# Loading an expert's matrices in two parts: w1 and w2 three tiles ahead, w3 two tiles ahead

## The chip, the cores and the metric

The kernel runs on one core of one Trainium2 chip. The metric is device time in microseconds (us) for one execution of the whole program; the time of a kernel is the median of its runs.

## What is computed

Two layers work on 3327 rows of 256 numbers. Each has an attention over a graph and a feed-forward part. The change lies in the feed-forward part of layer 0, a mixture of 16 experts of which each row uses the best two. Cut to that part, the reference is:

```python
logits = x @ gate_w + gate_b
top_probs, top_idx = top_k(softmax(logits), 2)          # two experts per row
top_probs = top_probs / sum(top_probs)
hidden = silu(x @ w1[e]) * (x @ w2[e])                   # w1, w2: 256 x 512 for each expert
y = hidden @ w3[e]                                       # w3: 512 x 256
x = x + sum over the two experts of top_probs * y
```

Before it stands layer 0's attention, after it layer 1's attention (softmax over the neighbours, times the projected rows) and a recurrence of 30 steps (tanh, sigmoid, layer norm, a 256 x 256 product).

## The kernel before, in words

The rows that go to one expert are listed and cut into tiles of 128. There are 61 tiles that are always done (`ALWAYS`). The first 16 (`FIRST`) are taken from lists of the first rows, while layer 0's attention and routing are still being finished; their tables are made by `find_tiles` (L670 on) from lists that GpSimd scatters into memory (`list_tokens`, L594). The other 45 come from the complete lists.

For each tile `s`, `work_off` (L909 on) does this. The tile's rows are gathered from memory by GpSimd (L775). They are needed with features first. For the early tiles TensorE transposes them (L804) and ScalarE copies the result to `hT` (L805). For tiles 19 to 60 (`by_dma`) the rows are split into halves of 16 bits by ScalarE (L784), written to memory by GpSimd (`asked`, L789) and read back by a transposing transfer of SyncE, the tile's `face` (L793), which is issued two tiles ahead in program order. Then TensorE makes `hT` times w1 and `hT` times w2 (`product`, L881: 32 matmul instructions), ScalarE and VectorE make `hidden` (L931, L939), and one tile later TensorE multiplies by w3 (`results`, L898: 8 matmul instructions). VectorE scales the result (L902) and GpSimd scatters it to memory (`given`, L903). Where faces are used, TensorE's products are tied to program order: w1 and w2 of tile `s`, then w3 of tile `s-1`.

The matrices of an expert are 3 times 512 KB. There are three sets of buffers (`SETS`): tile `s` uses set `s % 3`. One set is `first_set`, the other two lie in the buffer `wh`. `weights(s)` (L829 on) is SyncE's: it reads the tile's expert number and a flag from a table into registers (L833), and issues the three transfers for w1, w2 and w3 (L841, L842, L843). From tile 3 on each is conditional: it is skipped where the set already holds that expert. Tiles are numbered so that the same expert comes back in the same set.

What sets SyncE's order around the change is the program's order and `issue_after(behind)`: the table read of a set stands behind the last transfer of the set before. In one turn of the loop in `work_off` the queue receives:

```python
if by_dma(s + 2):
    face(s + 2)
if s + SETS - 1 < s1:
    weights(s + SETS - 1)      # w1, w2 and w3 of tile s + 2
```

SyncE works in order. A transfer that refills a buffer waits there until TensorE has read it: w3 of tile `s+2` waits for the results of tile `s-1`, as both use the same set. w1 and w2 of that set were read one tile earlier. Each transfer also waits until the eighth transfer before it (they take turns on eight completion counts, with ScalarE's) has landed.

At the start, set 0 is issued during attention (`begin_tiles`), and set 1 once attention has read the buffer `wh`.

Of the kernel before, what the change touches and what calls it, by code (L numbers as in the profile page):

```python
# [21 lines left out]
P = 128  # L22
# [9 lines left out]
def gat_moe_gat_recurrent_ffn(ctx: ExitStack, tc: tile.TileContext, a: dict, out: bass.AP):  # L32
    nc = tc.nc
# [338 lines left out]
    def score_vectors():  # L372

        for k in range(KD):
            for s in range(2):
                tc.keep_in_program_order(
                    nc.vector.scalar_tensor_tensor(
                        prod, wv1[:, k, 2:], 1.0, va[:, s, :], op0=ALU.mult, op1=ALU.mult,
                        accum_out=wv1[:, k, s : s + 1],
                    )  # L380
                )

    with ExitStack() as moe:
# [28 lines left out]
        with ExitStack() as pre:  # L412
# [58 lines left out]
            behind = None  # L471
# [9 lines left out]
            for ts in groups0[1:3]:  # L481
                behind = take_graph(ts, behind)
# [150 lines left out]
        SETS = 3  # L633
# [133 lines left out]
        def by_dma(s):  # L767
            return FIRST + 3 <= s < ALWAYS
# [28 lines left out]
        def features_first(s):  # L797
            if by_dma(s):
                return faces_of.pop(s)
            row = gotten.pop(s)  # L800
            pt = ps_o.tile([P, 512], F32, name="acc0")[:, :D].rearrange("p (k q) -> p k q", k=KD)
            hT = turn.tile([P, 2, KD, P], F32, name="hT")[:, 0]
            for k in range(KD):
                nc.tensor.transpose(pt[:, k, :], row[:, k * P : (k + 1) * P], ident)  # L804
            nc.scalar.copy(hT, pt)  # L805
            return hT

        behind = None
# [15 lines left out]
                m[:, 2 * third :].rearrange("p (f d) -> p f d", f=FH),  # L824
            )

        ew = {}

        def weights(s):  # L829
            nonlocal behind  # L830

            with tc.issue_after(behind) if behind else ExitStack():
                e, new = nc.values_load_multi_w_load_instructions(  # L833
                    table[0:1, 0:2, s], engines=[mybir.EngineType.SP], min_val=0, max_val=E - 1,
                    skip_runtime_bounds_check_because="numbers of experts, and 0 or 1",
                )[1]
            kw = {} if s < SETS or s in fresh else {"cond": new}
            if s < SETS:
                ew[s] = matrices(s)
            w1, w2, w3 = ew[s % SETS]  # L840
            nc.sync.dma_start(w1, a["w1"][bass.ds(e, 1)].rearrange("e (k p) h -> p (e k) h", p=P), **kw)  # L841
            nc.sync.dma_start(w2, a["w2"][bass.ds(e, 1)].rearrange("e (k p) h -> p (e k) h", p=P), **kw)  # L842
            behind = nc.sync.dma_start(w3, a["w3"][bass.ds(e, 1)].rearrange("e (f p) o -> p (e f) o", p=P), **kw).ins  # L843

        def recurrence_parameters(bank):

# [62 lines left out]
        def work_off(s0, s1, aside):  # L909

            nonlocal tied
            parameters = layer1_parameters()
            hT = features_first(s0)
            made = None
            for s in range(s0, s1 + 1):
                tied = by_dma(s)
                if s == FIRST:
                    for _ in aside:
                        pass
                if s == FIRST + 8:  # L920
                    score_vectors()
                hidT = made
                if s == 1:

                    results(0, hidT)
                if s < s1:
                    for q in range(s + 4 if s <= FIRST else s + 5, min(s + (5 if s < FIRST else 6), s1)):
                        gathered(q)
                    pa = product(hT, ew[s % SETS][0])
                    act, room = edge("e")  # L930
                    silu = nc.scalar.activation(act, pa, AF.Silu).ins  # L931
                    if by_dma(s + 4):
# [6 lines left out]
                    nc.vector.tensor_tensor(made, act, pb, ALU.mult)  # L939
                    if s + 1 < s1:  # L940
                        hT = features_first(s + 1)
                if s > max(s0, 1):
                    results(s - 1, hidT)
                if by_dma(s + 2):
                    face(s + 2)
                if s + SETS - 1 < s1:
                    weights(s + SETS - 1)
                next(aside, None)

        def begin_tiles():  # L950
# [9 lines left out]
        )  # L960
        gathered(3)
        weights(1)


# [19 lines left out]
        fresh = range(ALWAYS, ALWAYS + SETS)  # L984
# [4 lines left out]
        behind = None  # L989
# [280 lines left out]
```

## Time and profile before

| what | value |
|---|---|
| runs of the kernel before | 1831.34, 1831.44, 1829.67 us; median 1831.34 |
| the profiled execution | 1831.93 us, span 1830.2 us, mean granted clock 0.996 |
| transfers | 252.98 MB, mean 138 GB/s |
| experts' stage, 388 to 495 us | TensorE busy 100.97 of 107.00 us, DMA share 0.74, 230 GB/s |
| experts' stage, 495 to 731 us | TensorE busy 236.00 of 236.00 us, DMA share 0.79, 211 GB/s |
| SyncE in 495 to 731 us, waiting at L843 for TensorE's results (L898) | 29.1 us, 23 times |

The span runs from the first to the last instruction on the chip; the profiled execution's own time is 1.7 us longer. All times of single instructions come from this one execution. "Busy" of TensorE (PE) covers pipelined matmuls, so it says that matmuls are in flight, not that they run at their peak. PEld is the loading of the stationary operand, beside PE. "SPq" in a row is SyncE's queue: the duration is that of issuing a transfer, not of moving the data. The DMA share is the mean busy share of the 16 transfer engines. A wait is put down to the instruction whose completion came last; "remote" means that the profile found no instruction to name. L-numbers are lines of the kernel before.

### The profile page before, as it was taken

Reading aid. Unit: us, or ns where it says so; the run is one execution under the profiler, and the core shown is the slowest. Engines: PE = TensorE matmul, PEld = TensorE weight load, DVE = VectorE, ACT = ScalarE, POOL = GpSimd, SP = SyncE. Lnnn points to the kernel's source line nnn. Section 1 sums busy time; section 2 is a strip of 40 time slices with the busy share of each in tenths; the row PEclk is TensorE's granted clock in tenths of the full one; section 3 lists DMA queues with packets and bytes.
Section 4 is the critical chain, followed back from the end, with each engine's and each line's share of the span. In section 5 each row is a group of like instructions: output and inputs, shape, how many; then the busy total and the mean of one; then the engine's idle time right before and its main releaser. Section 6 shows DMA issues by size and latency. Waiting matters only on the chain.

```text
span 1830.2 us, 32461 instructions
## 1 busy us (share of the span) xinstructions
PE 1778.3 (97%) x10896; PEld 1622.7 (89%) x10896; DVE 1318.7 (72%) x4039; ACT 1229.7 (67%) x1587; POOL 914.0 (50%) x702
## 2 busy tenths in 40 slices
PE   6999999999999999799999999999999999999998
PEld 6999999898999999688888878888888888888887
DVE  6888888853222222657676679999999999999998
ACT  2877667642122121456666579999999999999994
POOL 3011212155454542101111028898889889888984
PEclk9999999999999999899999999999999999999999
DMA  8897360257696876400000037777777777767777
GB/s 174 119 125 85 73 102 15 67 168 207 218 264 186 220 203 164 154 15 16 18 22 14 12 91 175 175 166 175 167 168 179 168 177 168 173 166 169 179 168 224
DMA packets 454531, 252.98 MB, mean 138 GB/s; under 512 B 327493, under 2 KB 426620, under 8 KB 454362
## 3 DMA queue, kind: packets, MB, share of 16 engines
q1 hardware_dynamic: 436226, 212.51, 47.1%
q0 software_dynamic: 13456, 33.60, 10.8%
q10 hardware_dynamic: 4680, 4.76, 0.8%
q8 instruction: 89, 1.46, 0.3%
q14 instruction: 80, 0.66, 0.1%
HBM read 168.19 MB, written 97.20 MB: 145 GB/s over the span
## 4 chain that ended last, share of the span: by engine, by line
PE 54%; DVE 4%; DMA 1%; issue 0%; ACT 0%; POOL 0%; SPq 0%; ACTq 0%; DVEq 0%; POOLq 0%
PE po L1177 35%; PE acc L286 14%; PE bank L1142 4%; DVE pT L281 1%; PE acc L163 1%; DMA old<-kept 1%; DVE x L1187 0%; DVE x L1027 0%; DVE stats L1121 0%; DMA given<-wh,to 0%; DVE x L1195 0%; DMA zT<-given 0%; DVE st L116 0%; POOL rstd L121 0%; DVE low L1061 0%
## 5 line engine op out<-in xcount | busy, mean ns | idle before, releaser
L276 ACT ACTIVATE e<-rb,minus,full 128x384 f32<-128x384 f32 (+3 forms) x494 | 399.2, 823 | 168.0 <-DVE pT L281 147.1
L1112 POOL TENSOR_TENSOR th<-th,x 128x1024 f32<-128x1024 f32 (+1 forms) x210 | 464.8, 2213 | 94.3 <-ACT th L1109 86.6
L281 DVE SCALAR_TENSOR_TENSOR pT<-e,part,adjT 128x384 f32<-128x384 f32 (+3 forms) x494 | 383.4, 782 | 118.3 <-PE acc L286 102.3
L1177 PE MATMUL po<-wc,adjT 128*128 128x256 f32 x1888 | 422.2, 379 | 0.0
L1177 PEld LDWEIGHTS po<-wc,adjT 128*128 128x128 f32 x1888 | 356.4, 190 | 47.6 <-DVE x L1187 0.3
L1187 DVE SCALAR_TENSOR_TENSOR x<-po,rr,bb 128x256 f32<-128x256 f32 x780 | 325.0, 477 | 61.6 <-PE po L1177 61.1
L286 PE MATMUL acc<-wh,pT 128*128 128x129 f32 x2704 | 310.7, 276 | 2.1 <-DVE pT L281 2.1
L286 PEld LDWEIGHTS acc<-wh,pT 128*128 128x128 f32 x2704 | 305.4, 192 | 3.2 <-DVE pT L281 2.5
L286 PE MATMUL acc<-s_wh,pT 128*128 128x257 f32 x1352 | 295.5, 381 | 4.0 <-DVE pT L281 4.0
L286 PEld LDWEIGHTS acc<-s_wh,pT 128*128 128x128 f32 x1352 | 255.8, 190 | 43.1 <-DVE pT L281 7.4
L1177 PE MATMUL po<-wc,zT 128*128 128x256 f32 x1232 | 281.0, 379 | 0.6 <-DVE x L1187 0.6
L1121 DVE BATCH_NORM_STATS2 stats<-z 128x6 f32<-128x256 f32 x780 | 274.0, 411 | 1.4 <-ACT z L1116 1.4
L1177 PEld LDWEIGHTS po<-wc,zT 128*128 128x128 f32 x1232 | 229.2, 190 | 29.6 <-issue 0.9
L1152 ACT COPY adjT<-z 128x1024 int16<-128x1024 int16 x236 | 235.2, 1044 | 4.8 <-DVE pT L281 2.0
L121 POOL TENSOR_TENSOR rstd<-ve,neg_half 128x4 f32<-128x4 f32 (+3 forms) x28 | 31.9, 1141 | 411.5 <-DVE ve L119 313.0
L1109 ACT ACTIVATE th<-x 128x1024 f32<-128x1024 f32 (+1 forms) x210 | 209.1, 996 | 28.9 <-DVE x L1187 23.8
L1132 POOL TENSOR_TENSOR rr<-rr,neg_half 128x4 f32<-128x4 f32 (+1 forms) x210 | 206.7, 984 | 26.4 <-DVE rr L1127 26.3
L1116 ACT ACTIVATE z<-th 128x1024 f32<-128x1024 f32 (+1 forms) x210 | 207.1, 986 | 8.3 <-POOL th L1112 2.3
L931 ACT ACTIVATE e<-bank 128x512 f32<-128x512 f32 x61 | 36.4, 597 | 241.0 <-issue 183.2
L939 DVE TENSOR_TENSOR pT<-e,bank 128x512 f32<-128x512 f32 x61 | 41.9, 687 | 190.8 <-PE bank L881 160.7
L903 POOL DMA_INDIRECT given<-wh,to x61 | 61.1, 1001 | 119.2 <-DVE wh L902 102.8
L594 POOL DMA_INDIRECT lists<-pair,ati x52 | 63.5, 1221 | 107.5 <-DVE ati L581 49.3
(202 smaller groups left out, 1731.9 us busy)
## 6 DMA issues: line engine op xcount, KB each, us to landing
wh<-in_w_dram SPq DMA_DIRECT2D x120, 512.0 KB
apart<-adjT SPq DMA_DIRECT2D x236, 256.0 KB
first_set<-in_w_dram SPq DMA_DIRECT2D x63, 512.0 KB
in_bytes<-in_adj_dram POOLq DMA_DIRECT2D x3, 2496.0 KB
asked<-e POOLq DMA_DIRECT2D x42, 128.0 KB
adjT<-apart SPq DMA_TRANSPOSE x236
x<-in_x_dram SPq DMA_DIRECT2D x6, 512.0 KB
kept<-x SPq DMA_DIRECT2D x8, 384.0 KB
```

The costliest lines, as they stand in the source:

```text
L276: nc.scalar.activation(e[:, : n * P], rb[:, : n * P], AF.Relu, scale=sc.full[:, j, h : h + 1], bias=sc.minus[:, j, h : h + 1],)
L281: masked = nc.vector.scalar_tensor_tensor(pT[:, : n * P], e[:, : n * P], sc.part[:, j, h : h + 1], adjT[:, j // 2, ts[0] * P : (ts[-1] + 1 ...
L286: nc.tensor.matmul(po[c], lhsT=pT[:, c * P : (c + 1) * P], rhs=wh[:, j, h, :], start=(j == 0 and c % per_bank == 0), stop=(j == NT - 1), s ...
L1109: self.put(nc.scalar.activation(self.th, self.hs, AF.Tanh, scale=1.0 / S))
L1112: self.put(nc.gpsimd.tensor_tensor(self.th, self.th, self.hs, ALU.add))
L1116: self.put(nc.scalar.activation(self.z, self.th, AF.Silu, scale=1.0 / S))
L1121: self.put(nc.vector.bn_stats(stats[:, j, :], self.z[:, j, :]))
L1132: self.put(nc.gpsimd.tensor_tensor(r, r, neg_half[:, : self.n], ALU.pow))
L1142: nc.tensor.transpose(pt[:, j, k, :], self.z[:, 2 * c + j, k * P : (k + 1) * P], ident)
L1152: self.put(nc.scalar.copy(parts[:, c : c + 2], halves[:, c : c + 2]))
L1177: nc.tensor.matmul(self.po[:, j, :], lhsT=self.zT(j, k), rhs=wc[:, k, :], start=(k == 0), stop=(k == KD - 1),)
L1187: nc.vector.scalar_tensor_tensor(self.hs[:, j, :], self.po[:, j, :], self.r[:, j : j + 1], bb, op0=ALU.mult, op1=ALU.add)
```

## The change

`weights(s)` is divided. `weights_in(s)` reads the table and issues w1 and w2; `weights_out(s)` issues w3, behind whatever the queue had last. In the loop, tile `s` now issues w1 and w2 of tile `s+3` as soon as its own two products and VectorE's product stand in the program, ahead of the face of tile `s+2`; w3 of tile `s+2` comes after that face. In the first turn the complete set of tile 2 is issued first. Buffers, counts of instructions and what is computed stay.

```diff
-        def weights(s):
+        def weights_in(s):
             nonlocal behind
 
             with tc.issue_after(behind) if behind else ExitStack():
...
-            kw = {} if s < SETS or s in fresh else {"cond": new}
+            chosen[s] = e, {} if s < SETS or s in fresh else {"cond": new}
             if s < SETS:
                 ew[s] = matrices(s)
-            w1, w2, w3 = ew[s % SETS]
+            kw = chosen[s][1]
+            w1, w2, _ = ew[s % SETS]
             nc.sync.dma_start(w1, ...)
-            nc.sync.dma_start(w2, ...)
-            behind = nc.sync.dma_start(w3, ...).ins
+            behind = nc.sync.dma_start(w2, ...).ins
+
+        def weights_out(s):
+            nonlocal behind
+            e, kw = chosen.pop(s)
+            w3 = ew[s % SETS][2]
+            with tc.issue_after(behind):
+                behind = nc.sync.dma_start(w3, ...).ins
+
+        def weights(s):
+            weights_in(s)
+            weights_out(s)
...
                     nc.vector.tensor_tensor(made, act, pb, ALU.mult)
                     if s + 1 < s1:
                         hT = features_first(s + 1)
+                    if s == s0:
+                        weights(s + SETS - 1)
+                    if s + SETS < s1:
+                        weights_in(s + SETS)
                 if s > max(s0, 1):
                     results(s - 1, hidT)
                 if by_dma(s + 2):
                     face(s + 2)
-                if s + SETS - 1 < s1:
-                    weights(s + SETS - 1)
+                if s > s0 and s + SETS - 1 < s1:
+                    weights_out(s + SETS - 1)
                 next(aside, None)
```

More of the change, by code (lines that the diff above doesn't have):

```diff
@@ L825, in matrices @@
             )
-        ew = {}
-        def weights(s):
+        ew, chosen = {}, {}
+        def weights_in(s):
             nonlocal behind
@@ L836, in weights @@
                 )[1]
-            kw = {} if s < SETS or s in fresh else {"cond": new}
+            chosen[s] = e, {} if s < SETS or s in fresh else {"cond": new}
             if s < SETS:
                 ew[s] = matrices(s)
-            w1, w2, w3 = ew[s % SETS]
+            kw = chosen[s][1]
+            w1, w2, _ = ew[s % SETS]
             nc.sync.dma_start(w1, a["w1"][bass.ds(e, 1)].rearrange("e (k p) h -> p (e k) h", p=P), **kw)
-            nc.sync.dma_start(w2, a["w2"][bass.ds(e, 1)].rearrange("e (k p) h -> p (e k) h", p=P), **kw)
-            behind = nc.sync.dma_start(w3, a["w3"][bass.ds(e, 1)].rearrange("e (f p) o -> p (e f) o", p=P), **kw).ins
+            behind = nc.sync.dma_start(w2, a["w2"][bass.ds(e, 1)].rearrange("e (k p) h -> p (e k) h", p=P), **kw).ins
+        def weights_out(s):
[3 more added lines that the diff above has]
+            with tc.issue_after(behind):
+                behind = nc.sync.dma_start(
+                    w3, a["w3"][bass.ds(e, 1)].rearrange("e (f p) o -> p (e f) o", p=P), **kw
+                ).ins
+        def weights(s):
+            weights_in(s)
+            weights_out(s)
         def recurrence_parameters(bank):
```

## The prediction

> **What bounds the kernel now.** I read the page first: TensorE is busy for 97% of the span.
>
> ```profile
> span 1830.2 us, 32461 instructions
> ...
> PE 1778.3 (97%) x10896; PEld 1622.7 (89%) x10896; DVE 1318.7 (72%) x4039; ACT 1229.7 (67%) x1587; POOL 914.0 (50%) x702
> ```
>
> The change touches one stage, the experts' 61 tiles (TensorE works on them from 388.7 to 731.3 us). So the second view is what TensorE waited for in that stretch, 388 to 731 us.
>
> ```profile
> engine line waited for: us in total, times, longest us
> PE bank L881 <- ACT hT L805: 6.0, 2, 3.8
> ```
>
> That is all: 6.0 us, at two places (2.22 us before tile 1, 3.75 us before tile 7), and neither names a load of matrices. From tile 17 on, 495 to 731 us, the stretches' busy times give TensorE 236.00 of 236.00 us. A tile takes it 5.30 us: 32 matmuls for w1 and w2 (3.57 us until the next start), 8 for w3 (1.73 us). A weight load that comes earlier can remove nothing there; one that pushes something else back can cost.
>
> The third view is the timeline of the second place.
>
> ```profile
> 426.34 0.07 SPq L843 DMA_DIRECT2D wh<-in_w_dram  x1
> ...
> 427.36 0.39 SPq L841 DMA_DIRECT2D wh<-in_w_dram  x1
> ...
> 428.57 0.70 SPq L842 DMA_DIRECT2D wh<-in_w_dram  x1
> ...
> 432.62 2.58 POOL L594 DMA_INDIRECT lists<-pair,ati  x1 [0.30 <-issue]
> 435.13 0.69 DVE L939 TENSOR_TENSOR pT<-e,bank 128x512 f32<-128x512 f32 x1 [8.30 <-remote]
> 435.16 0.37 ACT L805 COPY hT<-acc 128x256 f32<-128x256 f32 x1 [5.21 <-remote]
> 435.19 0.37 SPq L843 DMA_DIRECT2D wh<-in_w_dram  x1
> ...
> 435.58 5.17 PE L881 MATMUL bank<-hT,wh 128*128 128x128 f32 x32 [3.75 <-ACT hT L805]
> ```
>
> VectorE, ScalarE and SyncE are released within 0.06 us of each other, by TensorE's count, which is raised at 435.04 although the matmuls that raise it are drawn as ended by 431.8. Tile 7's matmuls then take 5.17 us, not 3.73. The busy times of 2 us stretches say what the transfers did meanwhile (columns: PE, PEld, DVE, ACT, POOL busy, clock, DMA share, GB/s):
>
> ```profile
> 426.00:428.00 2.00, 2.00 (x19) 1.97 (x18) 0.48 (x1) 0.00 (x0) 1.43 (x2) 1.00 0.06 9
> 428.00:430.00 2.00, 2.00 (x20) 2.00 (x20) 0.00 (x0) 0.60 (x1) 1.47 (x2) 1.00 0.94 16
> 430.00:432.00 2.00, 1.83 (x9) 1.27 (x8) 0.00 (x0) 0.00 (x0) 1.62 (x2) 1.00 0.63 241
> ```
>
> The transfer engines go from idle (0.06) to full (0.94) at only 16 GB/s: the first packets of w1 for tile 8, issued at 427.36 between the scatters of L594, take 2.2 to 3.0 us each in the trace, later ones 0.08. The two earlier skipped sets (tiles 6 and 7) had left the engines idle.
>
> [...] idle 3.75 us, then clock 0.5 for 3.41 us. [...] a face issued right after a w3 load landed 1.0 to 1.5 us after that load, not before it.
>
> **The change part by part.** *Added and removed instructions:* none that compute; the same 61 sets, 183 loads. The order of instructions on VectorE, ScalarE and GpSimd is unchanged; on TensorE one transpose (L804) of an early tile moves behind 16 matmuls, about 0, since both run back to back. What moves is SyncE's order. Per tile it was: face(s+2), table, w1, w2, w3 of set s+2. It becomes: table, w1, w2 of set s+3, face(s+2), w3 of set s+2.
>
> *w1 and w2 earlier.* They have to wait for tile s's own two products, whose buffer they refill, and then have over 10 us. In the trace before, from tile 20 on, w1 landed 1.0 to 5 us ahead of its use. The slack becomes some 8 us. Worth nothing by itself, as TensorE waited for no w1 there; only one wait of 0.22 us for a w2 (402.57, tile 2) is found between the matmuls at all, and tile 2's set is loaded as before.
>
> *w3 later in the queue.* It is issued about where it was (after the results of tile s-1), used 14 us later. Nothing.
>
> *The read of the lists* (L686, once). It stood ahead of w1 and w2 of tile 11 and now stands behind them: 1 MB, some 3 us at the 376 GB/s that the stretch from 392 to 408 us shows. It landed at 457.8 by the records, and TensorE first uses it at 460.79: slack 3.0. As the sets before it also leave earlier, I take 0; at worst 2 us.
>
> *The face later.* This is the cost. SyncE now stands at w2 of set s+3 until tile s's second product is counted: 3.75 us after the tile's start (521.13 by the count for the tile begun at 517.38). Queued behind it are the face, then w3; tile s+2's first matmul waits for the face. From w2 to the next issue took 0.17 us (skipped) or 0.47 us (loaded), by w3 and face in the rows below, and w2 itself starts about 0.1 us after its count.
>
> ```profile
> 517.38 3.73 PE L881 MATMUL bank<-face,first_set 128*128 128x128 f32 x32
> ...
> 518.03 0.37 SPq L843 DMA_DIRECT2D wh<-in_w_dram  x1
> 518.50 1.21 SPq L793 DMA_TRANSPOSE face<-asked  x1
> ```
>
> So the face goes out at +4.0 to +4.3 us; before, here, at +1.1. It is needed at +10.6. Its lead falls from a median of 10.24 us (all 42 faces against the tile's first matmul) to 6.6, or 6.3 behind a real load. How long it takes, from the records of completion counts: 2.5 to 4 us in tiles without a load, where 2.6 us are left over; 5 to 7.6 us behind a load (10 of 41 took over 6.3 us). With a load it now stands behind w1 (issued about 2 us before w2, not 0.8) and w2 (0.47 us before), but no longer behind w3 as well. Before, w2 landed a median 5.1 us after its issue and the face about 1.2 us after the load ahead: 3.85 + 5.1 + 1.2 = +10.15 against +10.6, slack 0.45; the wider spacing of w1 and w2 gives back up to 0.8. Sixteen tiles load. Of the 20 landings of w2 on record since 470 us, three took over 5.1 + 0.45 + 0.8 = 6.35 us (7.22, 7.48, 8.12): together 3.8 us late. All three close a run of loads in successive tiles (35 to 37, 58 to 60), whose first sets now start a tile earlier. I take +1.0 us; the ends are 0 and +8.3 (landings as slow as before: the excess over 6.3 us, summed over those ten).
>
> *The early stall.* w1 of tile 8 can start once tile 5's first product is done, 422.0, w2 about 424.8; before it was 427.36. w1 of tile 9 follows at about 428.1 (tile 6's product), before 437.05. So at 428 the transfer engines are at work on w2 of tile 8 (about 5 us to land), and the burst no longer begins from idle amid the scatters. If that is what held the count, the wait of 3.75 us goes, and with it the slow clock, 5.17 - 3.73 = 1.44 us: -5.2 us. What is late next is tile 7's own row (there since the transposes at 429.7), so nothing. The trace does not show why a burst should hold TensorE's count, so this is bounded by 0 and -5.2, and above zero by a second hold of the same size, +5.2, as more loads now fall into 422 to 433. I take -5.2. The wait of 2.22 us at tile 1 stays: its loads are not moved.
>
> *Sum.* -5.2 + 1.0 = -4.2 us. Against the profiled execution: span 1830.2 to 1826.0, its time 1831.93 to 1827.7 (1.7 us lie outside the span). The median of the runs is 1831.34, 0.6 below that execution, so 1827.1.
>
> **The rivals.** (a) *Forecast:* the stall goes, faces are nearly always in time: 1827.1, by itself 1825 to 1829. (b) *A stall takes the place of the one removed:* w1 of tile 9 begins at 428.1, 0.7 us after the load that stalled; the scatters go on to 432.6, and the count is held again. For it: the other hold, at 390.5 to 393.7, also began with a burst of loads. Then 1831.3 + 1.0 = 1832.3, which is also the time if the change does nothing that TensorE sees. (c) *Slower, faces too late:* the mechanism is SyncE standing at w2 for 3.75 us with the face behind it; it decides once a face takes over 6.3 us. With the landings of before, +8.3 us and the early stall kept: 1839.6; half of it, 1835.5. Against it: w3 no longer stands ahead of the face.
>
> **How the numbers follow.** Chances: (a) 0.47, (b) 0.31, (c) 0.22. A measurement of this kernel tells about 0.2% from no change, 3.7 us: faster is below 1827.7, slower above 1835.0. Of (a) 0.05 lies inside; of (c) 0.02; of (b) 0.02 is slower. Faster 0.42, same 0.36, slower 0.22. The range 1825.0 to 1836.5 leaves out 0.04 of (a) and about 0.13 of (c); both signs are in it, and (a)'s own is above.
>
> **What would show it.** Right: no TensorE wait over 1 us at tile 7, clock 1.00 from 434 to 438, w1 of tile 8 issued near 422, faces at about +4.2 us in each tile, waits for faces of 0 to 2 us in all. Wrong: TensorE idle before L894 (the product's new line) released by a face, several times from 495 us on, is (c); a wait of 3 us or more anywhere from 425 to 440 is (b). The prediction fails altogether if the stage from 495 to 729 us gets shorter: nothing there was waiting.

## The result, and the profile after

The changed kernel takes 1849.53 us (median of 5 runs, 1845.54 to 1853.17) against 1831.34 us: ratio 1.0098, 95% interval 1.0083 to 1.0112. It is slower by 18.2 us where 4.2 us less were forecast. Two later sets of runs gave 1.0083 (1.0066 to 1.0100) and 1.0113 (1.0097 to 1.0130).

The profiled execution after is the shortest of its runs (1845.54 us). The head of its page:

```profile
span 1843.8 us, 32567 instructions
...
PE 1782.0 (97%) x10896; PEld 1623.3 (88%) x10896; DVE 1327.6 (72%) x4039; ACT 1229.2 (67%) x1587; POOL 914.2 (50%) x702
```

The same instructions that compute, a span that is 13.6 us longer. Laying the two lists of matmuls over each other, one by one, shows where TensorE falls behind: -0.2 us at the start of tile 17, +8.2 at tile 60, still +8.3 at the first product of the recurrence, +13.6 at its last. (The -0.2 hides a small loss: the first tile starts 1.0 us earlier in this profile, and tiles 0 to 17 take 0.8 us longer.) So two places lose most, and one of them is not in the experts' stage at all.

First, what TensorE waited for among the experts, 388 to 739 us:

```profile
engine line waited for: us in total, times, longest us
PE bank L894 <- issue: 9.1, 6, 4.5
PE bank L894 <- ACT hT L805: 2.1, 1, 2.1
PE bank L894 <- DMA face<-asked: 0.8, 1, 0.8
```

L894 is the product's new line. 12.0 us instead of 6.0, and a face is named. "issue" means that the profile saw nothing to wait for, so those six have to be looked up. The longest is the early stall, one tile earlier than before (timeline from 420 us):

```profile
421.11 0.39 SPq L842 DMA_DIRECT2D wh<-in_w_dram  x1
...
427.64 0.38 SPq L843 DMA_DIRECT2D wh<-in_w_dram  x1
427.72 0.69 DVE L952 TENSOR_TENSOR pT<-e,bank 128x512 f32<-128x512 f32 x1 [4.97 <-remote]
...
429.12 0.37 ACT L805 COPY hT<-acc 128x256 f32<-128x256 f32 x1 [7.40 <-remote]
...
429.54 5.46 PE L894 MATMUL bank<-hT,first_set 128*128 128x128 f32 x32 [4.52 <-issue]
```

w1 of tile 8 is issued at 421.11, as the prediction wanted; w2 has to wait until 427.64 for a count that TensorE raises 4.6 us after the drawn end of the matmuls it stands for (423.07). VectorE and ScalarE are held as well, tile 6 starts 4.52 us late, and its matmuls take 5.46 us. The stretches (PE, PEld, DVE, ACT, POOL busy, clock, DMA share, GB/s) show that the transfer engines were nearly idle in the middle of this hold:

```profile
426.00:428.00 2.00, 0.00 (x0) 0.00 (x0) 0.28 (x1) 0.00 (x0) 1.54 (x2) 1.00 0.01 1
428.00:430.00 2.00, 0.46 (x4) 0.46 (x5) 0.41 (x1) 0.37 (x1) 1.55 (x2) 1.00 0.42 28
430.00:432.00 2.00, 2.00 (x13) 2.00 (x12) 0.00 (x0) 0.00 (x0) 1.70 (x2) 0.58 0.44 68
```

Next, the first faces (timeline from 500 us):

```profile
500.55 1.46 SPq L793 DMA_TRANSPOSE face<-asked  x1
501.07 3.73 PE L894 MATMUL bank<-hT,first_set 128*128 128x128 f32 x32
...
509.21 5.25 PE L894 MATMUL bank<-face,wh 128*128 128x128 f32 x32 [2.68 <-issue]
```

By the completion counts the face of tile 19, issued at 500.55, landed at 509.13, 8.58 us later; tile 19 starts 0.09 us after that. Of the 42 faces, six made TensorE wait 0.2 us or more (tiles 19, 21, 25, 34, 46, 58; 5.4 us together), and with the first wait (2.68 us) the granted clock falls to 0.50, from 508.82 to 512.23 us: 3.73 us of matmuls take 5.25. Each late face belongs to a tile `k` for which the set of tile `k+1` is really loaded: then w1 and w2 of that set went out just ahead of it. Behind such a pair the median landing is 5.9 us (16 faces), otherwise 3.1 us (24). And five of the six late faces (19, 21, 25, 34, 46) went out at +5.0 to +5.8 us of their tile, not at +4.0 to +4.3: SyncE stands at w2 until TensorE's count comes, and in about every third tile from 17 to 50 that count comes some 1 us after the drawn end of the second product.

SyncE's wait has moved as foreseen, from w3 to w2 (its queue's waits, 495 to 739 us):

```profile
SPq L843 <- PE bank L894: 29.4, 31, 2.2
SPq L842 <- PE bank L894: 9.8, 13, 1.4
```

The second place is the recurrence, whose code the diff doesn't touch. Two views of it after; in the second, the row of L1144 has to be read against GpSimd's row above it:

```profile
1514.18 1.66 DVE L1204 SCALAR_TENSOR_TENSOR x<-po,rr,bb 128x256 f32<-128x256 f32 x4 [0.38 <-issue]
```

```profile
1652.49 1.66 DVE L1204 SCALAR_TENSOR_TENSOR x<-po,rr,bb 128x256 f32<-128x256 f32 x4 [0.79 <-PE po L1194]
...
1655.49 2.36 POOL L1129 TENSOR_TENSOR th<-th,x 128x1024 f32<-128x1024 f32 x1
1655.78 2.10 DVE L1144 TENSOR_SCALAR rr<-v 128x4 f32<-128x4 f32 x1
```

And the same step before:

```profile
1643.88 1.66 DVE L1187 SCALAR_TENSOR_TENSOR x<-po,rr,bb 128x256 f32<-128x256 f32 x4 [0.44 <-PE po L1177]
...
1647.16 0.17 DVE L1127 TENSOR_SCALAR rr<-v 128x4 f32<-128x4 f32 x1
1647.25 2.36 POOL L1112 TENSOR_TENSOR th<-th,x 128x1024 f32<-128x1024 f32 x1
```

Before, VectorE's small addition (the epsilon) begins 0.09 us ahead of GpSimd's addition and takes 0.17 us. After, it begins 0.29 us behind it and is held until GpSimd is done: 2.10 us. This happens four times from 1656 to 1675 us (1.99 to 2.10 us), and each time the held addition ends 0.02 to 0.04 us after GpSimd's. Why VectorE is held there is not shown. What pushes VectorE over is a gap in its own stream: at 1514.18 it starts 0.38 us late with nothing to wait for. Such a gap stands at three steps of the recurrence. The third is in the row of 1652.49, which is 0.79 us late where the same row before (1643.88) is 0.44, and the first held addition is in the step right behind it. Before, there is no such gap at these steps.

### The profile page after: what moved, and what is told of

The parts are those of the page before. It is cut to its first block, busy times and chain, and to the rows that moved or that the text cites. A ratio compares the mean times of both kernels' runs of the same rounds, so it can differ in the third digit from the quotient of the medians.

```text
span 1843.8 us, 32567 instructions
## 1 busy us (share of the span) xinstructions
PE 1782.0 (97%) x10896; PEld 1623.3 (88%) x10896; DVE 1327.6 (72%) x4039; ACT 1229.2 (67%) x1587; POOL 914.2 (50%) x702
## 4 chain that ended last, share of the span: by engine, by line
PE 79%; DVE 7%; issue 4%; DMA 2%; POOL 2%; ACT 1%; another core or an unknown queue 0%; SPq 0%; POOLq 0%; DVEq 0%; ACTq 0%
PE po L1194 34%; PE acc L286 23%; PE bank L894 10%; PE acc L911 5%; PE bank L1159 3%; DVE pT L281 3%; PE acc L163 1%; PE bank L148 1%; DVE x L1204 1%; PE bank L528 1%; DMA old<-kept 1%; DVE stats L1138 0%; POOL rstd L121 0%; POOL given L916 0%; DMA given<-wh,to 0%
```

## The theory, its rivals, and a table of all profiles

Theory after the result: two losses. (1) A face now goes out at about +4.3 us, behind w1 and w2 of a later set, and with a real load ahead it needs longer than the 6.3 us that are left. (2) The recurrence falls into a slower beat because VectorE's instructions stand shifted by one. Rivals: loads three tiles ahead crowd the transfer engines by themselves; SyncE's standing at w2 is enough; the early half of the split makes or lengthens the hold between tiles 5 and 8; the recurrence differs by chance from execution to execution.

The table has one profile per kernel (starts of tiles and products; tile 17 starts where the late half of the split begins) and the timed runs, each beside the kernel before on the same chip. "VectorE" is the number of its instructions ahead of the recurrence.

| kernel | tile 17 starts | tiles 17 to 60 | recurrence | VectorE | median us | ratio |
|---|---|---|---|---|---|---|
| before | 495.78 | 228.30 | 739.05 | 2193 | 1831.34 | 1 |
| after | 495.55 | 236.74 | 744.40 | 2192 | 1849.53 | 1.0098 |
| after, second set | 489.44 | 243.15 | 743.52 | 2192 | 1843.83 | 1.0083 |
| face first | 490.82 | 228.12 | 744.12 | 2192 | 1831.92 | 1.0019 |
| early sets only | 489.86 | 229.55 | 738.64 | 2193 | 1827.27 | 0.9997 |
| face late, two ahead | 487.90 | 233.47 | 739.19 | 2193 | 1830.95 | 1.0021 |
| face first, filler | 496.23 | 228.38 | 738.75 | 2193 | 1835.48 | 1.0017 |
| faces three ahead | 495.53 | 230.30 | 738.50 | 2193 | 1834.60 | 1.0010 |
| no late loads | 495.75 | 228.12 | 743.92 | 2192 | 1838.92 | 1.0032 |
| face from ScalarE | 496.08 | 237.36 | 738.29 | 2193 | 1844.00 | 1.0071 |
| after, filler | 500.27 | 240.45 | 739.00 | 2193 | 1847.99 | 1.0087 |
| before, one less | 495.58 | 228.72 | 744.06 | 2192 | 1839.85 | 1.0047 |
| early only, again | 495.68 | 230.59 | 739.46 | 2193 | 1834.14 | 1.0008 |
| late only, face first, filler | 499.90 | 228.37 | 738.62 | 2193 | 1835.09 | 1.0011 |
| after, third set | 495.50 | 240.25 | 743.92 | 2192 | 1851.74 | 1.0113 |
| after, filler, again | 497.75 | 237.79 | 739.43 | 2193 | 1846.03 | 1.0078 |
| late only | 494.43 | 238.16 | 743.77 | 2192 | 1844.38 | 1.0064 |
| first seven faces first | 489.76 | 230.41 | 739.02 | 2193 | 1830.02 | 1.0005 |
| parameters late | 492.94 | 241.21 | 738.55 | 2193 | 1842.24 | 1.0077 |

## Experiments on the faces

**The face ahead of w1 and w2.** Everything else as in the changed kernel:

```diff
+                    if by_dma(s + 2):
+                        face(s + 2)
                     if s + SETS < s1:
                         weights_in(s + SETS)
...
-                if by_dma(s + 2):
-                    face(s + 2)
```

> The changed kernel, but each face is put into SyncE's queue ahead of w1 and w2 of the set three tiles on, as before the change. Late faces (theory): the 8.4 us that TensorE lost from tile 17 on come back, so 236 us of 236 busy there; the early hold near 425 to 436 us stays as in the changed kernel (about 6 us with its slow clock), so 1831 to 1835. Contention (rival): what costs is that sets three tiles ahead put more transfers in front of everything; then faces still land late and most of the 8 us stays, 1839 or more.

Measured: 1831.92 us, ratio 1.0019 (1.0011 to 1.0026). In the profile no tile from 17 to 60 waits; the stage is back at 228.12 us, with all loads three tiles ahead. So loads three tiles ahead cost this stage nothing; the face's place behind them does. What is left, 4.1 us, is no more than what the recurrence loses (744.12, 5.1 us over the profile before).

**The face late, but loads two tiles ahead.** The order of before (face between w2 and w3), the face made to wait for the tile's second product:

```diff
-                    if s == s0:
-                        weights(s + SETS - 1)
-                    if s + SETS < s1:
-                        weights_in(s + SETS)
                 if s > max(s0, 1):
                     results(s - 1, hidT)
+                if s + SETS - 1 < s1:
+                    weights_in(s + SETS - 1)
                 if by_dma(s + 2):
-                    face(s + 2)
-                if s > s0 and s + SETS - 1 < s1:
+                    face(s + 2, second)        # waits for this tile's second product
+                if s + SETS - 1 < s1:
                     weights_out(s + SETS - 1)
```

> Sets two tiles ahead as before, w1, w2 and w3 of tile s+2, but the face of tile s+2 stands between w2 and w3 and waits for tile s's second product, as it does in the changed kernel. This is the delay of the face without the earlier loads. Late faces: a lead of about 6.5 us as in the changed kernel, so 5 to 9 us lost from tile 19 on, 1837 to 1841, while the early part is as before. Contention: without sets three tiles ahead nothing is lost, 1831 to 1833.

Measured: 1830.95 us, ratio 1.0021 (1.0013 to 1.0028), stage 233.47 us. Issued at +3.76, with w1 and w2 out some 3 us ahead of it, three faces wait (tiles 37, 48, 43; 1.89, 0.77 and 0.10 us). The median is 3.2 us above the kernel before on this chip, below the 1837 to 1841 expected. A late face alone costs some (5.2 us of the stage in this profile), not the 8 to 15 us of the changed kernel.

**The changed kernel once more, in the same set.**

> The changed kernel once more, for a second profile: its five runs spread from 1845.5 to 1853.2, and the profiled one was the fastest. Late faces: again 8 us from tile 17 on, and the rest of the loss is to be found in this profile. If the losses from tile 17 on are much greater here, these faces explain the spread; if the recurrence loses again (4.7 us near 1650 us in the first profile), it is there.

Measured: 1843.83 us, ratio 1.0083. In its profile the face of tile 19 took 14.11 us and tile 19 waited 7.46; tile 25 waited 2.25. The stage is 243.15 us. There is no hold between tiles 5 and 8 in any of the four profiles of this set.

**Faces three tiles ahead,** at the same place in the queue:

```diff
-                if by_dma(s + 2):
-                    face(s + 2)
+                if by_dma(s + 3):
+                    face(s + 3)
```

> The changed kernel with every face issued three tiles ahead instead of two, at the same place in the queue, behind w1 and w2; the buffers stay three, since the face of tile s+3 refills what tile s's products have just read. Theory (the face is late because a lead of 6.3 us is less than it needs behind a pair of loads): the lead is 11.6 us, no wait for a face, tiles 17 to 60 in 228 to 229 us; what remains is the recurrence's part, 3 to 5 us, so 1830 to 1833, unless VectorE's count of instructions moves. Rival (the loads three tiles ahead cost by themselves, by crowding the transfer engines): waits remain, for faces or for other transfers, 233 us or more for the stage, 1836 or more.

Measured: 1834.60 us, ratio 1.0010 (1.0004 to 1.0017); stage 230.30 us. One face waits, that of tile 20: it took 13.05 us, more than even this lead. Otherwise the lead is ample (least margin after tile 24: 2.65 us). The stage is 1 us above the 228 to 229 expected, because of that one face. The theory holds; the rival (crowding by itself) does not, except at that one place.

**No loads in the late part.** `table[:, 1]`, the flag, is made zero for the tiles from 16 on:

```diff
-                table[:, 1, s1 : s0 + n], table[:, 0, s1 : s0 + n], table[:, 0, s1 - SETS : s0 + n - SETS], ALU.not_equal
+                table[:, 1, s1 : s0 + n], table[:, 0, s1 : s0 + n],
+                table[:, 0, s1 : s0 + n] if s0 else table[:, 0, s1 - SETS : s0 + n - SETS], ALU.not_equal
```

> The changed kernel with every load of matrices for the tiles from 17 on left out: the flag that says that a set holds another expert is made zero, so all transfers of w1, w2 and w3 are skipped (those tiles then work with the matrices of earlier tiles). SyncE's order and its wait at w2 stay. Theory (a face needs to be late and to stand behind loads): faces go out at about +4 us as in the changed kernel, land in 2.4 to 4 us, no wait for them, tiles 17 to 60 in 228 us, time 1828 to 1832. Rival (the standing at w2 is enough): waits for faces remain, stage 232 us or more.

Measured: faces go out at +3.94 to +5.44, land in 2.3 to 4.7 us, and nothing waits: stage 228.12 us. SyncE's standing at w2 is by itself harmless. The time, 1838.92 us (1.0032, 1.0020 to 1.0044), missed the expected 1828 to 1832: this chip's kernel before stands at 1832.62, and the recurrence lasts 743.92.

**The face from ScalarE's queue,** at the same moment:

```diff
-            nc.sync.dma_start(
+            put = nc.scalar.dma_start(
                 faces_of[s].bitcast(I16), put_down.pop(s)..., transpose=True
             )
+            tc.add_manual_dep(put.ins, behind.name, ...)   # the tile's second product
```

> The changed kernel with the face issued by ScalarE instead of SyncE, and made to wait for the tile's second product, so that it goes out at about the same moment (+3.8 to +4.5 us) but in another queue than w1 and w2. If the order inside SyncE's queue is what makes the face late, it lands in 3 to 4 us, tiles 17 to 60 take 228 to 230 us and the time is 1829 to 1833. If the bytes of w1 and w2 delay it whichever queue it comes from, landings stay at 5 to 8 us behind real loads and the stage at 235 us or more, time 1838 or more. ScalarE's own standing should cost nothing: its work for the tile is done by then.

Measured: 1844.00 us, ratio 1.0071 (1.0048 to 1.0094), stage 237.36 us. Its waits from 495 to 735 us:

```profile
PE bank L899 <- issue: 3.5, 2, 2.8
PE bank L899 <- DMA face<-asked: 2.5, 2, 1.5
PE bank L899 <- ACT hT L810: 1.5, 1, 1.5
```

Faces behind real pairs still took 5.4 to 8.1 us, that of tile 19 10.9. So it is not the order inside SyncE's queue: the megabyte of w1 and w2 that is under way delays the face from whichever queue it comes.

**The first seven faces alone put first** (tiles 19 to 25; the rest stays behind w1 and w2):

```diff
+                    if by_dma(s + 2) and s + 2 < FIRST + 10:
+                        face(s + 2)
                     if s + SETS < s1:
                         weights_in(s + SETS)
...
-                if by_dma(s + 2):
+                if by_dma(s + 2) and s + 2 >= FIRST + 10:
                     face(s + 2)
```

> The changed kernel with the first eight faces alone (tiles 19 to 26) put ahead of w1 and w2; the faces from tile 27 on stay behind them. VectorE's stream has the old length, so the recurrence should last 739 us. In the five profiles of the changed kernel and of it with the VectorE instruction added, tile 19 waited 2.7 to 7.5 us and tiles 21 to 25 another 0.3 to 2.7; tiles 27 to 60 waited 0.5 to 1.2 us in all. Theory (most of the faces' loss is made at the start of the stage, where three gathers of rows per tile and ScalarE's loads of layer 1's parameters share the transfer engines): stage of tiles 17 to 60 in 229 to 230.5 us, ratio 1.001 to 1.003. Rival (the loss is spread over all loading tiles): stage of 233 us or more, ratio 1.004 or more.

(`FIRST` is 16, so the edit moves seven faces and not the eight of the expectation.) Measured: 1830.02 us, ratio 1.0005 (0.9997 to 1.0014), stage 230.41 us; three faces wait later, 1.03 us in all. So most of the loss is made at the start of the stage. (The ratio is a little below the 1.001 to 1.003 expected.)

**Layer 1's parameters loaded six tiles later:**

```diff
-                if s == FIRST + 8:
+                if s == FIRST + 14:
                     score_vectors()
...
-                    if FIRST <= s < ALWAYS:
+                    if FIRST + 6 <= s < ALWAYS:
                         next(parameters, None)
```

> The changed kernel with ScalarE's loads of layer 1's parameters (512 KB in all in the first three) and what VectorE makes of them begun six tiles later, so that they no longer meet the first faces. If these loads are what makes w2 of tile 20 and the face of tile 19 take 9 to 14 us, that face lands in 6 to 8 us, tile 19 waits under 1.5 us and the stage falls to 230 to 234 us. If the three gathers per tile and the loads of w1 and w2 suffice, the wait at tile 19 stays at 2.7 to 7.5 us and the stage at 236 us or more. VectorE's count of instructions may come out as either length; the recurrence is taken out by its own time (739 or 744 us).

Measured: tile 19 waits 1.84 us (8.48 us landing) instead of 2.7 to 7.5, but the stage is 241.21 us and the ratio 1.0077 (1.0063 to 1.0090): the long wait has moved to tile 25. Timeline from 518 us, and 536 to 548 us for the last row, which shows only what lies in that window:

```profile
530.15 0.36 ACTq L368 DMA_DIRECT2D va<-in_ga_dram  x1
...
531.84 0.37 SPq L843 DMA_DIRECT2D wh<-in_w_dram  x1
532.31 4.07 SPq L793 DMA_TRANSPOSE face<-asked  x1
...
545.84 2.47 PE L894 MATMUL bank<-face,wh 128*128 128x128 f32 x10 [7.01 <-DMA face<-asked]
```

That face took 13.39 us, 2.2 us behind the load of `va` (one row copied into all partitions, 256 KB), as in the changed kernel's second set the face of tile 19 took 14.11 us, 2.15 us behind the same load. What was issued from 529.6 to 532.3, on every queue, landed only 9 to 13 us later. The expectation that tile 19 improves and the stage shrinks was half wrong: the collision follows the parameters. The other profiles say the same. In all seven in which a face behind a real pair goes out 2.1 to 2.8 us after `va`, it took 10.6 to 14.1 us; in the changed kernel's first profile, 1.15 us after it, 8.58. Which of the three first parameter loads matters is not shown: they are 256 KB each (768 KB, not the 512 KB of the expectation), and the third, `fW`, follows 2.4 to 4.8 us behind the face in all seven.

## Experiments on the recurrence

**The face first, and VectorE given one instruction more:**

```diff
     nc.vector.memset(neg_half, -0.5)
+    nc.vector.memset(neg_half, -0.5)
```

> The face ahead of w1 and w2 again, as in the run with the face first, and one more VectorE instruction near the start (the constant of -0.5 is written twice). In the three profiles with the split over all tiles VectorE ran 2192 instructions before the recurrence and 2735 in it; in the three others 2193. In the former, three gaps of 0.33 us stand at VectorE's instructions 533, 1557 and 2069 of the recurrence (distances of 1024 and 512); after the third, the addition of the epsilon (0.17 us) starts behind GpSimd's addition and takes 2.0 us, four times, and the recurrence's products last 743.5 to 744.4 us instead of 738.6 to 739.2. Theory: the gap belongs to a place in VectorE's instruction stream, [...] and what it hits is a matter of the count before it. With one instruction more, the recurrence's products last about 739 us, no addition of epsilon over 1.5 us, and the time is about 1828 (ratio 0.999 to 1.001). Rival: the loss comes from something else that the split leaves behind (SyncE's longer stream, the later transfers): 744 us and 1832 again.

Measured: the recurrence lasts 738.75 us and no addition of epsilon takes over 1.5 us. That part holds. The ratio, 1.0017 (1.0009 to 1.0025), did not return to 1. The profile has a hold of 4.51 us at tile 6, which no profile of the earlier set had; whether that is what is left is not shown.

**The kernel before, with one VectorE instruction less.** Nothing of the change is in it:

```diff
-    nc.vector.memset(neg_half, -0.5)
+    nc.gpsimd.memset(neg_half, -0.5)
```

> The kernel before, with nothing of the change, but with one VectorE instruction less: the constant of -0.5 is written by GpSimd instead. Theory: VectorE has 2192 instructions ahead of the recurrence, the gaps of 0.33 us stand at its instructions 533, 1557 and 2069, the epsilon's addition is held for 2.0 us four times, and the recurrence lasts 743.5 to 744.4 us: ratio 1.002 to 1.0035. Rival (the count has nothing to do with it): 738.3 to 739.2 us, ratio 0.9995 to 1.0005.

Measured: recurrence 744.06 us, and this is what TensorE waits for in it (before: 0.6 us at L1177):

```profile
PE po L1177 <- DVE x L1187: 4.5, 5, 1.4
```

The ratio is 1.0047 (1.0033 to 1.0061), more than the expected 1.002 to 1.0035; 5.0 us (0.27%) is the recurrence, the rest of its profile's 7.9 us lies mainly in layer 1's attention (2.6 us). That stretch, from tile 60 to the recurrence, differs by up to 3.7 us (357.8 to 361.5) among the nineteen profiles, so a single profile doesn't settle a sum to the microsecond; why it differs is open.

Over all nineteen profiles the rule has no exception: 2192 instructions, 743.5 to 744.4 us (seven profiles); 2193, 738.3 to 739.5 us (twelve). In the first kind the gap of about 0.35 us stands at VectorE's instructions 533, 1557 and 2069 of the recurrence, in the second at none of these. The instruction that is missing in the changed kernel is a wait: ahead of the multiplication of layer 1's projection with `va`, VectorE waited before for the load of the projection's vectors (`wv1`) by an instruction of its own, at 533.49 us, and after it does not. With the face first it is another wait that is missing, at 741.5 us in the profile before. So it is the number that counts, not which instruction; that the split changes the number because it deals out the eight completion counts in another order is likely, but not shown. The gaps stand 1024 and 512 instructions apart, and behind each of them, by 1.0 to 1.9 us, a transfer of 8 KB starts in the trace's instruction queue (where the stream has its old length, one starts 1.0 to 2.4 us ahead of that place). What makes the gaps is not shown.

## Experiments on the sum and on the early half

**The early half alone,** on two chips (the sets from tile 19 on loaded as before):

```diff
-                    if s + SETS < s1:
+                    if s + SETS < s1 and s < FIRST:
                         weights_in(s + SETS)
...
                 if s > s0 and s + SETS - 1 < s1:
+                    if s > FIRST:
+                        weights_in(s + SETS - 1)
                     weights_out(s + SETS - 1)
```

> The split with w1 and w2 three tiles ahead only for the first 16 tiles (sets up to 18); from tile 17 on the order of the kernel before. Late faces: nothing is lost from 495 us on, only the early hold of about 6 us (before: 5.2 us) remains, so 1831 to 1834. If the early part were the greater cost (rival), it would stay near 1845.

> The split for the early sets alone (up to the set of tile 19) once more, as in the run with the early part alone, which gave 0.9997 and showed no hold of TensorE between tiles 5 and 8; nor did the three other profiles taken with it. All four taken later showed one (1.0 to 4.5 us). If the split has no part in the hold: ratio 0.999 to 1.001, and a hold in the profile as in the others of this set. If, as the prediction had it, the split takes the hold away: ratio near 0.997. If it makes it longer (4.5 us and 1.7 us of slow clock, against 3.75 and 1.4 before): ratio 1.0005 to 1.0015. VectorE's stream has its old length, so the recurrence lasts 739 us.

Measured: 0.9997 (0.9987 to 1.0007), then 1.0008 (1.0000 to 1.0016). In the first profile there is no hold, in the second there is one of the old size:

```profile
434.10 6.56 PE L894 MATMUL bank<-hT,wh 128*128 128x128 f32 x32 [3.85 <-ACT hT L805]
```

The early half takes nothing away. On its own it also adds nothing, or at most 0.16%. In the second profile part of what is over is not the early half's: tile 24 waits 2.23 us for its w2, which this kernel loads two tiles ahead. In other executions the old order has waits that a load three tiles ahead could remove; the profile before happened to have none.

**The late half alone, face first, with the filler.** The early sets are loaded as before, by `weights(s + 2)` at the old place up to tile 16, and the first pair that goes out earlier is that of tile 19:

```diff
-                    if s + SETS < s1:
+                    if s > max(s0, FIRST) and s + SETS < s1:
                         weights_in(s + SETS)
...
-                if s > s0 and s + SETS - 1 < s1:
-                    weights_out(s + SETS - 1)
+                if s + SETS - 1 < s1:
+                    if s <= max(s0, FIRST):
+                        weights(s + SETS - 1)
+                    else:
+                        weights_out(s + SETS - 1)
+                if s == max(s0, FIRST):
+                    weights_in(s + SETS)
```

> The split for the late sets alone (from the set of tile 20 on), with the face ahead of w1 and w2, and with one more VectorE instruction near the start, so that its stream has its old length; the early sets are loaded as before. Against the run with the face first and the same instruction added (ratio 1.0017), it lacks only the early split. Theory (what is left there belongs to the early part, a longer hold between tiles 5 and 8): 0.9993 to 1.0007, stage of tiles 17 to 60 in 228 to 229 us. Rival (loads three tiles ahead cost something in the late part even with the face first): 1.001 or more.

Measured: 1.0011 (1.0003 to 1.0018), above the expected band. The stage is 228.37 us, so the late half with the face first costs nothing there. In its profile what is over comes before tile 17 (499.90), from holds that this kernel has with the early order of before:

```profile
429.05 5.46 PE L895 MATMUL bank<-hT,first_set 128*128 128x128 f32 x32 [1.85 <-issue]
...
439.41 5.47 PE L895 MATMUL bank<-hT,wh 128*128 128x128 f32 x32 [2.27 <-ACT hT L806]
```

**The changed kernel with the filler,** alone and then on one chip with the changed kernel and with the late half alone (the edit above, without the face first and without the filler).

> The changed kernel, whole, with one more VectorE instruction near the start (the constant of -0.5 written twice). The changed kernel's VectorE stream is one instruction shorter than before: an operation of layer 1's parameters waits for one completion count instead of two, because the split moved SyncE's transfers among the eight counts. Theory (the loss has two parts, late faces and the shifted VectorE stream): the recurrence's products last 738 to 739.2 us (743.5 to 744.4 in the changed kernel), tiles 17 to 60 still 236 to 243 us with waits for faces; the ratio is 1.0083 to 1.0098 less 5 of 1830 us, so 1.0055 to 1.0071. Rival (the recurrence's loss comes from the lateness of what goes before): 744 us again and 1.008 or more.

Measured: recurrence 739.00, stage 240.45, but ratio 1.0087 (1.0072 to 1.0101), above the expected 1.0071: this profile has a hold of 6.72 us before tile 6, and tile 17 starts at 500.27. Hence the comparison on one chip:

> The changed kernel once more, to be compared on one chip with the two that follow. Expected: ratio 1.008 to 1.010, tiles 17 to 60 in 236 to 243 us, recurrence 743.5 to 744.4 us.

> The changed kernel with one more VectorE instruction near the start, again, now beside the changed kernel on the same chip. Theory (late faces and shifted VectorE stream add up): 5 us (0.27%) less than the changed kernel's third run, recurrence 739 us, stage unchanged at 236 to 243 us. Rival (the two parts are not additive, the earlier 1.0087 being the true value): the same ratio as the changed kernel within 0.1%.

> The split for the late sets alone, in the changed kernel's own order (face behind w1 and w2), with the early sets loaded as before; VectorE's stream is as short as in the changed kernel. If the early split has no part in the loss: the changed kernel's ratio within 0.1%, stage 236 to 243 us. If the early split costs (a longer hold between tiles 5 and 8): 0.1 to 0.25% below the changed kernel. If the early split helps, as the prediction had it: up to 0.3% above.

Measured: the changed kernel 1851.74 us, 19.9 over before; with the filler 1846.03, 5.7 less; the late half alone 1844.38, 7.4 less. The first difference is mainly the recurrence's (743.92 against 739.43 us), as expected. The second was not: alone the early half costs nothing, together with the late half 7.4 us (intervals 1.0113, 1.0097 to 1.0130, and 1.0064, 1.0049 to 1.0080). What TensorE waited for from tile 17 on, in the changed kernel's third profile and in the late half alone (experts' lines):

```profile
PE bank L894 <- issue: 8.0, 2, 7.4
PE bank L894 <- DMA face<-asked: 0.8, 1, 0.8
```

```profile
PE bank L894 <- issue: 3.3, 3, 2.0
PE bank L894 <- DMA face<-asked: 1.9, 1, 1.9
...
PE bank L894 <- ACT hT L805: 1.2, 1, 1.2
```

The longest wait, 7.4 us before tile 19, is as long as the difference of the medians by chance only. Without the early half that tile waits 0.68 us, but tiles 18, 21 and 25 wait 1.2 to 2.0 us each, and the stages of the two profiles differ by 2.1 us (240.25 and 238.16), the executions by 3.8. What does differ at tile 19 is the order: its face goes out 2.75 us after `va` in the changed kernel and 0.15 us ahead of it in the late half alone, and takes 13.28 and 6.36 us. It seems that the early half shifts which loads meet the first faces; that this makes the 7.4 us of the medians is not shown.

No kernel of the study is faster than before. The early half alone (0.9997 and 1.0008) and the kernel with the first faces put first (1.0005) can hardly be told from it.

**Where the early hold belongs.** The profiles were taken in five sets, each on one chip, besides the first two. All profiles of three sets have a hold between tiles 5 and 8, like the first two; the six profiles of the other two have none (in the table: face first; early sets only; face late, two ahead; after, second set; and in the later set: first seven faces first; parameters late). The chip alone doesn't decide it: one set with the hold and one without bear the same chip number. A second sign goes with it. In the thirteen profiles with the hold TensorE's count for the second product comes about 1 us late in nearly every third tile from 20 to 50, where GpSimd issues gathers and a scatter back to back. In the six without, that pattern is missing, though GpSimd issues the same; each has at most four late counts, and not at those places. The kernel before is a little faster in the sets without the hold as well: its medians are 1827.78 and 1829.54 us there, and 1831.34 to 1832.62 elsewhere. Why counts come late is open.

## Why the prediction was wrong

- *"w1 and w2 earlier" and "w3 later": right as far as they went.* In the profile after no late tile waits for w1, w2 or w3; no time was won. That they were worth "nothing by itself" left out what they do to others on the way. (One reading is too narrow: in the profile before, a face issued right after w3 lands mostly 0.6 to 1.5 us behind it, not 1.0 to 1.5. It does land behind it.)
- *"The read of the lists": right.* Nothing waits for it in the profile after; in the second set's profile there is one wait of 0.5 us, inside the bound of 2.
- *"The face later": the step that failed, in size.* The mechanism is as written: SyncE stands at w2, and the face behind it comes too late. The +1.0 us taken for it measured 8.4 us in the first profile and 9.5 to 14.9 in the next four of the changed kernel with and without the filler. The middle came out: out at +4.3 us (median) and landing 5.6 to 5.9 us later behind a real pair (medians of the five profiles) is about +10.2, against +10.15 forecast. The tail did not. The prediction counted three late faces at the ends of runs of loads (37, 58 to 60). The late ones are above all 19, 21 and 25, with 6 to 14 us, where the parameters of layer 1 are loaded as well, which the sum leaves out. The moment was wrong for them too: the +3.75 us to TensorE's count was read from one tile, but in the same profile before it is 4.5 to 5.2 us in every third tile from 20 to 50, which takes up to 1.4 us off the lead of 6.3. In the second set those counts are in time, and the stage still lost 14.9 us, so the landings weigh more. That +8.3 of rival (c) is the price of the first profile is luck: its sum was over ten other faces, evenly spread.
- *"The early stall": failed.* -5.2 was taken because a load begun earlier would keep the transfer engines busy. They were empty again at 426 us (share 0.01), and the hold came back one tile earlier: 4.52 us and 1.73 us of slow clock (granted 0.50 from 430.31 to 433.72 us), 6.25 in place of 5.2. That is the effect of rival (b), but not at its place: w1 of tile 9 had not begun. The term is +1.05 us instead of -5.2. The hold appears with the early order of before and with the new one, and is missing with either in whole sets of runs. So it isn't made by when w1 of tile 8 starts. Its cause stays open.
- *A term that is not in the sum: the recurrence, +5.35 us.* The prediction said that the order of instructions on VectorE is unchanged, and the description of the change that their counts stay. That holds for the instructions that compute, but a wait fell away: 2193 became 2192. None of the rivals had it.
- *"Sum":* 8.4 + 5.35 - 0.2 (up to tile 17) is the 13.6 us of the span in the profile. The median is 4 us above that execution; the spread of the stage from profile to profile (236.7 to 243.2 us) would cover it, but those executions have no profile.

## What to carry to other kernels

A small transfer that something waits for should go out ahead of bulk loads that have time, not behind them: the same loads with the face ahead cost the stage nothing (228.12 us against 228.30 before, and 236.74 with the face behind them). When a lead is cut, price the landing with what will then be in flight, including other engines' one-time loads, and not with the landings of the old order. And look at the whole span after moving transfers: waits are instructions, and one fewer made a tightly timed loop that begins 500 us later take 5 us more.

## What the runs showed of the hardware that was not expected

- One VectorE instruction more or less ahead of the recurrence decides between 739 and 744 us, in nineteen of nineteen profiles, through gaps of about 0.35 us at places 512 or 1024 instructions apart.
- An addition on 4 numbers per partition (0.17 us) is held up to 2.10 us when GpSimd's addition has begun 0.29 us earlier.
- A face of 128 KB takes 2.3 to 4.7 us with no loads of matrices about; behind two loads of 512 KB 5.6 to 5.9 (medians), from the same queue as from another; with a load of one row into all partitions begun 2.1 to 2.8 us ahead of it as well, 10.6 to 14.1 in seven of seven.
- TensorE's count can come late, by about 1 us in every third tile or so and with a hold of up to 6.7 us between tiles 5 and 8, in all profiles of one set of runs and in none of another, whatever the kernel.
- With a wait of TensorE of 2.68 us (changed kernel, tile 19) the granted clock fell to 0.50 for 3.41 us, as long as with waits of 3.75 us (before, tile 7) and 4.52 us (changed kernel, tile 6); a wait of 2.22 us (before, tile 1) left it at 1.00.
